# Two graph layers on 32 batches: other first and last work, scalings apart from additions, GpSimd's additions in another order

## The chip, the cores and the metric

The kernel runs on one core of a Trainium2 chip. TensorE (PE) multiplies matrices into PSUM; VectorE (DVE), ScalarE (ACT) and GpSimd (POOL) work on tiles in SBUF; SyncE (SP) and ScalarE issue the transfers. Each engine works through its own list of instructions in order and waits at an instruction until its inputs and its buffer are free. The metric is the device time of one execution in microseconds, lower is better.

## The reference

For 32 batches b, with x[b] of 512 nodes × 512 features and one adjacency matrix for all:

```python
# layer 0: attention with 8 heads of 64, then residual and layer norm
q, k, v = (x @ W + bias).reshape(b, n, 8, 64)        # for Wq, Wk, Wv
scores = einsum('bihd,bjhd->bhij', q, k) / 8
weights = softmax(scores + where(adj == 0, -1e9, 0))
x = layernorm(x + einsum('bhij,bjhd->bihd', weights, v))
# layer 1: graph convolution, then residual and layer norm
deg = adj.sum(axis=1)
norm_adj = adj * deg[:, None]**-0.5 * deg[None, :]**-0.5
x = layernorm(x + norm_adj @ (x @ W1) + b1)
```

## The kernel before

The program is one long list. Every instruction on TensorE, VectorE, ScalarE and GpSimd is pinned to its place (class InOrder), so the code's order is each engine's order; the recording helper is line 44, and the profile puts L44 to nearly everything. Work is therefore told apart by the names of its tiles.

The main loop (746 to 853) goes over S = 128 blocks k. A block is one batch b and one pair g of heads, in the order ORDER = (0, 2, 1, 3). A block makes scores in PSUM (tile sc, TensorE), VectorE subtracts the mask (e<-sc,maskT), ScalarE takes the exponential (e<-e), GpSimd adds the e tiles of a head pair for the denominators (acc<-e and acc<-acc,e, accumulate, 360), and TensorE multiplies e with v (tile av, values, 379). av is transposed by VectorE into yb, and four DMAs set it into the batch's tile YT (name yT; of the last batch wv, which is free by then). The denominators are folded by VectorE (fold, folded) and inverted once per batch (inverse_all: a product with spread, four copies into inv, one RECIPROCAL).

Beside the four blocks of batch b runs the rest, on a list called side: the projections of batch b+1, what finishes batch b-1, and its convolution. Projections use a seven-product scheme (seven, 257): seven products of quarter matrices, each of which VectorE adds to what came before. Their sums go through tiles e1 (name e), u2 (name u) and the outputs v or kq. The products of one scheme go through a PSUM pool of three buffers (name mm). In values_of (286) the fourth product's sum u2 gets the value bias from GpSimd (u<-u,bv_r, in middle), and VectorE's v and the next products' sums follow. x comes as 8 row strips per half (load_x, 105) into a tile that VectorE transposes (turn, 118) to XT; combine makes four differences of it. Weights are loaded as 32-row pieces (load_parts, 146) and get four differences (weigh, 167: wv and wk on GpSimd).

finish (464) scales the values by inv on VectorE (yT<-yT,inv), adds the residual on GpSimd (yT<-yT,xr; both in add, 503), takes mean and variance (measure), their root on GpSimd (rstd), normalises on ScalarE (norm), and splits the result into a high part hi (ScalarE) and a low part lo (VectorE: lo<-yT,dis,hi), both rounded for a faster product; then GpSimd adds b1 (yT<-yT,b_r; both in split, 548). convolve (579) multiplies hi and lo with adjT (first for all batches but the last, block for the last), makes a second seven-product scheme with W1 (second, 623), whose sums extend (660) completes on GpSimd for the batch before the last, then statistics and store.

The dict beside (794 to 800) says which of the finishing work stands behind which of the projection's products; cut deals the list to the four blocks. The second accumulation pair of a block is deferred: it is put on pending, and put_off (more, 741) takes one from there at a place in the list; what is left goes at the head of the next block. So the place of put_off in beside decides where GpSimd's acc<-acc,e stands:

```python
2: put_off, 3: rest[3:4], 4: rest[4:5] + put_off,
```

Product 3 is the one whose sum u2 GpSimd adds the bias to; the number is the position in the list of products, and what is listed there comes behind that product.

Before the loop stand the loads (176 to 192), wv's and wk's differences, the turn of batch 0, its values, the masks (adjacency, 215: transposition of adj by TensorE, a mask, a copy adjT on VectorE, a comparison of the two (off) and its sum (lost)) woven into its keys and queries. Behind the loop come the last batch's late scalings (pairs), the last convolution and stores (855 to 884). The last two blocks take their shares from lines 814 to 823; the last batch's accumulations go into wq, wk, wv and XT, which are free by then.

Of the kernel before, what the change touches and what calls it, by code (L numbers as in the profile page):

```python
# [9 lines left out]
F32 = mybir.dt.float32  # L10
# [39 lines left out]
def unshifted(  # L50
# [54 lines left out]
    def load_x(b, j):  # L105


        if b == 0 and j == 1:
# [9 lines left out]
    def turn(b, j):  # L118
# [4 lines left out]
        if j == 0 and b:  # L123
            load_x(b, 1)

# [20 lines left out]
    def load_parts(w, name, engine):  # L146
        t = consts.tile([P, 7, 2, HALF], F32, name=name)
        for i in range(2):
            for q in range(4):
                engine.dma_start(  # L150
                    t[32 * q : 32 * (q + 1), 2 * i : 2 * i + 2].rearrange("r j u o -> r (j u) o"),
                    w[ts(q, P), ts(i, HALF)].rearrange("(t r) o -> r t o", r=32),
                )
        return t
# [20 lines left out]

    load_x(0, 0)
    load_x(0, 1)
    wv = load_parts(Wv, "wv", nc.scalar)
    bv_r = load_row(bv, "bv_r", nc.scalar)
    bk_c = load_column(bk, "bk_c")  # L180
    bq_c = load_column(bq, "bq_c")
    wk = load_parts(Wk, "wk", nc.sync)
# [9 lines left out]
    b1_r = load_row(b1, "b1_r", nc.sync)  # L192

# [20 lines left out]

    def adjacency(m):
# [6 lines left out]
        vector.tensor_copy(adjT[:, m, :], p)  # L222
        off = work.tile([P, N], F32, name="off", tag="e", bufs=6)
        vector.tensor_tensor(off, p, adjT[:, m, :], ALU.not_equal)
        vector.tensor_reduce(lost[:, m : m + 1], off, AX.X, ALU.add)
# [153 lines left out]
    def values(s):  # L379
# [13 lines left out]
        if jj == 0:  # L393
            return

# [11 lines left out]
        for q in range(4):  # L407
            queue = scalar if q > 1 and (b, g) == blocks[-1] else nc.sync
            queue.dma_start(
# [54 lines left out]
    def finish(b):  # L464
# [38 lines left out]
        def add(i):  # L503
# [5 lines left out]
            gpsimd.tensor_add(y, y, R[b][i])  # L509

        def add_pair(i, g):

            y, r = YT[b][:, i, :], R[b][i]
            for h in (2 * g, 2 * g + 1):
                at = slice(h * HD, (h + 1) * HD)
                vector.scalar_tensor_tensor(
                    y[:, at], y[:, at], t["inv"][:, i, h : h + 1], r[:, at], op0=ALU.mult, op1=ALU.add
                )
# [648 lines left out]
```

## Time and profile before

| | us |
|---|---|
| median of 3 runs | 2893.41 (2891.94 to 2895.27) |
| profiled execution | 2891.81 |
| its span, first to last instruction | 2890.0 |
| TensorE's mean granted clock | 0.995 |
| first block's scores on TensorE start at | 56.83 |
| last block's scores on TensorE start at | 2825.51 |
| one exponential on ScalarE (e<-e, 128x1024) | 1.057 |
| one accumulation on GpSimd (acc<-acc,e) | 2.373 |
| one yT<-yT,inv on VectorE, mean of 124 | 1.216 |
| one yT<-yT,xr on GpSimd, mean of 124 | 1.589 |
| one lo<-yT,dis,hi on VectorE, mean of 124 | 1.272 |

A row of the timeline is start, length, engine, line, operation, output<-inputs with partitions x elements and type, how many in a row were joined, and in brackets the idle time before it and what ended that. Where several are joined, the length is that of the whole row, gaps in it included. PE is TensorE's products, PEld its weight loads. A view of waits has total, number and longest of an engine's idle times by what released it. A row by stages has the stretch, its length, and the busy time of each engine in it with the number of instructions, the granted clock of TensorE as a share of full speed, the share of time that the 16 DMA engines moved data, and GB/s.

### The profile page before, as it was taken

What the parts mean: (1) busy time and instruction counts of PE and PEld (TensorE: products, weight loads), DVE (VectorE), ACT (ScalarE), POOL (GpSimd) and SP (SyncE); (2) the same over time, 40 slices, a digit from 0 to 9 for tenths busy, and PEclk for the clock granted to TensorE, in tenths of its full rate; (3) what the DMA queues carried; (4) which work ended last, traced back from release to release, by engine and by line L of the source; (5) the groups of instructions that cost most, each with busy time, mean ns of one, the idle gap of its engine ahead of it and who ended that gap; (6) DMA issues with size and microseconds to landing.
All of it is one profiled execution on the core that took longest, in us unless ns stands there. A gap on an engine that the chain in (4) does not pass through costs nothing.

```text
span 2890.0 us, 34431 instructions
## 1 busy us (share of the span) xinstructions
PE 2813.2 (97%) x12408; PEld 1867.5 (65%) x12408; DVE 2292.3 (79%) x3205; ACT 1041.4 (36%) x1312; POOL 1844.5 (64%) x1174
## 2 busy tenths in 40 slices
PE   7999999999999999999999999999999999999997
PEld 5566666666666666666666666666666666666655
DVE  6688778788778887787887788877878877888787
ACT  1243333333333433333333334333333333343343
POOL 3566666666666666666666666666666666666665
PEclk9999999999999999999999999999999999999999
DMA  5111222111221112221112211222211122112211
GB/s 131 22 30 48 55 55 44 41 48 48 59 55 41 36 48 55 55 44 41 48 48 59 55 41 35 50 55 55 44 41 48 48 59 56 40 35 50 56 36 53
DMA packets 383396, 142.35 MB, mean 49 GB/s; under 512 B 280048, under 2 KB 349680, under 8 KB 383216
## 3 DMA queue, kind: packets, MB, share of 16 engines
q1 hardware_dynamic: 380720, 138.35, 20.2%
q10 hardware_dynamic: 2496, 1.70, 0.3%
q8 instruction: 100, 1.64, 0.2%
q14 instruction: 80, 0.66, 0.1%
HBM read 72.88 MB, written 33.55 MB: 37 GB/s over the span
## 4 chain that ended last, share of the span: by engine, by line
PE 81%; DVE 11%; POOL 3%; ACT 2%; issue 1%; DMA 0%; SPq 0%; DVEq 0%; POOLq 0%
PE mm L44 49%; PE sc L44 17%; PE av L44 16%; DVE e L44 3%; DVE st L44 2%; ACT y L44 2%; DVE v L44 1%; POOL u L44 1%; POOL rstd L44 1%; DVE mv L44 1%; DVE u L44 1%; DVE yb L44 0%; DVE kq L44 0%; DMA x<-in_x_dram 0%; DVE lo L44 0%
## 5 line engine op out<-in xcount | busy, mean ns | idle before, releaser
L44 ACT ACTIVATE e<-e 128x1024 f32<-128x1024 f32 x512 | 540.7, 1057 | 1164.7 <-DVE e L44 1139.7
L44 POOL TENSOR_TENSOR acc<-acc,e 128x1024 f32<-128x1024 f32 x248 | 588.5, 2373 | 187.3 <-ACT e L44 182.5
L44 DVE SCALAR_TENSOR_TENSOR e<-sc,maskT 128x1024 f32<-128x1024 f32 x512 | 597.5, 1207 | 24.9 <-PE sc L44 24.5
L44 PE MATMUL sc<-kq 64*128 64x512 f32 x2048 | 517.8, 618 | 3.6 <-DVE e L44 3.5
L44 PE MATMUL mm<-xT,wk 128*128 128x256 f32 x1792 | 472.8, 386 | 2.3 <-DVE off L44 1.0
L44 POOL TENSOR_TENSOR acc<-e 128x1024 f32<-128x1024 f32 x126 | 297.1, 2358 | 271.8 <-ACT e L44 271.8
L44 PE MATMUL av<-e,v 128*64 128x512 f32 x2048 | 467.9, 598 | 0.0
L44 PE MATMUL mm<-xT,wq 128*128 128x256 f32 x1792 | 459.9, 379 | 0.0
L44 PE MATMUL mm<-wv,xT 128*128 128x256 f32 x1792 | 408.1, 385 | 49.2 <-DVE e L44 37.9
L44 PEld LDWEIGHTS mm<-wv,xT 128*128 128x128 f32 x1792 | 338.1, 192 | 123.8 <-PE mm L44 33.8
L44 PEld LDWEIGHTS mm<-xT,wk 128*128 128x128 f32 x1792 | 329.8, 190 | 125.6 <-issue 70.1
L44 PEld LDWEIGHTS mm<-xT,wq 128*128 128x128 f32 x1792 | 340.5, 190 | 46.3
L44 PEld LDWEIGHTS sc<-kq 64*128 64x128 f32 x2048 | 173.3, 186 | 284.9 <-issue 156.3
L44 PEld LDWEIGHTS av<-e,v 128*64 128x64 f32 x2048 | 135.5, 136 | 316.2 <-issue 292.4
L44 POOL TENSOR_TENSOR yT<-yT,xr 128x512 f32<-128x512 f32 x124 | 193.4, 1589 | 78.1 <-DVE yT L44 78.1
L44 PE MATMUL mm<-w,zT 128*128 128x256 f32 x992 | 224.6, 379 | 0.0
L44 POOL TENSOR_TENSOR rstd<-ve,minus_half 128x4 f32<-128x4 f32 (+1 forms) x66 | 66.3, 1005 | 243.4 <-DVE nmu L44 243.4
L44 DVE TENSOR_TENSOR kq<-u,mm 128x512 f32<-128x512 f32 x128 | 87.7, 685 | 157.7 <-PE mm L44 154.2
L44 POOL TENSOR_TENSOR yT<-yT,b_r 128x512 f32<-128x512 f32 x124 | 171.5, 1394 | 56.4 <-DVE lo L44 56.4
L44 PEld LDWEIGHTS mm<-w,zT 128*128 128x128 f32 x992 | 188.2, 190 | 27.0 <-issue 1.5
L44 PE MATMUL mm<-adjT,lo 128*128 128x512 f32 x496 | 198.2, 400 | 5.6 <-DVE lo L44 5.6
L44 PE MATMUL mm<-adjT,hi 128*128 128x512 f32 x496 | 203.6, 410 | 0.0
(131 smaller groups left out, 3360.0 us busy)
## 6 DMA issues: line engine op xcount, KB each, us to landing
x<-in_x_dram SPq DMA_DIRECT2D x256, 128.0 KB, 2.9
out_dram<-y SPq DMA_DIRECT2D x127, 256.0 KB, 2.1
xr<-in_x_dram SPq DMA_DIRECT2D x124, 256.0 KB, 3.3
yT<-yb SPq DMA_DIRECT2D x496, 64.0 KB, 2.4
wv<-in_L_gnn_Wv_dram ACTq DMA_DIRECT2D x8, 128.0 KB, 4.8
wk<-in_L_gnn_Wk_dram SPq DMA_DIRECT2D x8, 128.0 KB, 4.1
wq<-in_L_gnn_Wq_dram SPq DMA_DIRECT2D x8, 128.0 KB, 4.8
yT<-in_adj_dram SPq DMA_DIRECT2D x1, 1024.0 KB, 6.8
```

The source lines that it names most:

```text
L44: return self.tc.keep_in_program_order(op(*args, **kwargs))
```

## The change

What it does, in the order of the code. Batch 0 is loaded as four row tiles of 256 KB, which stay as its residual; TensorE turns them by products with the unit matrix (turn_first), copied to XT by VectorE and ScalarE. The pieces of wv go between these tiles, half on SP's queue, half on ScalarE's; both halves of batch 1's x are loaded before the loop. adjacency leaves two copies to ScalarE, and the comparison (compare) goes to the blocks 3 and 4 of the loop. Five of the seven value products of batch 1 go into block 0.

In the steady state add becomes scale and add, and split becomes low and lift: the four scalings are listed ahead of the four additions, the low parts ahead of the additions of b1, and the first two put_off stand behind product 3 and at 5. In the list of instructions of each engine this leaves TensorE, VectorE and ScalarE as they were for batches 2 to 31; on GpSimd one deferred accumulation moves behind the value bias: before acc, u, acc, four yT, after u, acc, acc, four yT.

At the end, the low parts of the batch before the last go ahead of and between other work in the last blocks, and two accumulations are put off behind them (within, and the pending list); the last block's values are copied by ScalarE and VectorE, turned by TensorE into PSUM (turn_values) and read from there by add_pair, without yb and its four DMAs; extend(2) and extend(3) are done at once for all, and the order of the last products of the batch before the last and of the closing list is another.

```diff
@@ -120,8 +120,21 @@
...
-        if j == 0 and b:
+        if j == 0 and b > 1:
...
+    def turn_first(j, i):
+        p = ps_mm.tile([P, 2, HALF], F32, name="mm")
+        for n in range(2):
+            for u in range(2):
+                for q in range(4):
+                    at = q * P + (2 * i + u) * 32
+                    tensor.matmul(
+                        p[32 * q : 32 * (q + 1), u, ts(n, P)], R[0][2 * j + n][:, at : at + 32], ident,
+                        start=True, stop=True,
+                    )
+        (scalar.copy if i else vector.tensor_copy)(XT[:, 2 * j + i], p)
     def combine(b, at):
@@ -173,13 +188,19 @@
...
-    load_x(0, 0)
-    load_x(0, 1)
-    wv = load_parts(Wv, "wv", nc.scalar)
-    bv_r = load_row(bv, "bv_r", nc.scalar)
+    R[0] = acts.tile([P, NT, D], F32, name="xr", tag="zT", bufs=1)
+    R[0] = [R[0][:, i, :] for i in range(NT)]
+    wv = consts.tile([P, 7, 2, HALF], F32, name="wv")
+    for i in range(2):
+        for k, engine in enumerate((nc.sync, nc.scalar)):
+            engine.dma_start(R[0][2 * i + k], x[0, ts(2 * i + k, P), :])
+            load_parts(Wv, "wv", engine, wv, [(i, 2 * k), (i, 2 * k + 1)])
+        if i == 0:
+            bv_r = load_row(bv, "bv_r", nc.scalar)
+    wk = load_parts(Wk, "wk", nc.sync)
...
-    wk = load_parts(Wk, "wk", nc.sync)
@@ -190,6 +211,9 @@
...
+    if B > 1:
+        load_x(1, 0)
+        load_x(1, 1)
@@ -212,6 +236,8 @@
...
+    plainT = acts.tile([P, NT, N], F32, name="plainT", tag="hi", bufs=1)
     def adjacency(m):
@@ -219,10 +245,13 @@
...
-        vector.tensor_copy(adjT[:, m, :], p)
-        off = work.tile([P, N], F32, name="off", tag="e", bufs=6)
-        vector.tensor_tensor(off, p, adjT[:, m, :], ALU.not_equal)
-        vector.tensor_reduce(lost[:, m : m + 1], off, AX.X, ALU.add)
+        scalar.copy(adjT[:, m, :], p)
+        scalar.copy(plainT[:, m, :], p)
+    def compare(m):
+        vector.tensor_tensor(plainT[:, m, :], plainT[:, m, :], adjT[:, m, :], ALU.not_equal)
+        vector.tensor_reduce(lost[:, m : m + 1], plainT[:, m, :], AX.X, ALU.add)
@@ -392,6 +421,12 @@
...
+        if (b, g) == blocks[-1]:
+            turned = work.tile([P, N], F32, name="avT", tag="yb", bufs=1)
+            scalar.copy(turned[:, :HALF], av[:, :HALF])
+            vector.tensor_copy(turned[:, HALF:], av[:, HALF:])
+            AV[b, g] = turned
+            return
@@ -405,8 +440,7 @@
...
-            queue = scalar if q > 1 and (b, g) == blocks[-1] else nc.sync
-            queue.dma_start(
+            nc.sync.dma_start(
@@ -500,21 +534,31 @@
...
-        def add(i):
+        def scale(i):
...
-            gpsimd.tensor_add(y, y, R[b][i])
+        def add(i):
+            gpsimd.tensor_add(YT[b][:, i, :], YT[b][:, i, :], R[b][i])
+        def turn_values(g):
+            t["y"] = ps_mm.tile([P, NT, P], F32, name="mm")
+            for i in range(NT):
+                tensor.transpose(t["y"][:, i], AV[b, g][:, ts(i, P)], ident)
         def add_pair(i, g):
...
-            for h in (2 * g, 2 * g + 1):
+            for k in range(2):
+                h = 2 * g + k
...
+                values = t["y"][:, i, ts(k, HD)] if (b, g) == blocks[-1] else y[:, at]
...
-                    y[:, at], y[:, at], t["inv"][:, i, h : h + 1], r[:, at], op0=ALU.mult, op1=ALU.add
+                    y[:, at], values, t["inv"][:, i, h : h + 1], r[:, at], op0=ALU.mult, op1=ALU.add
...
         def measure(i):
@@ -545,12 +589,13 @@
...
-        def split(i):
-            x1 = YT[b][:, i, :]
+        def low(i):
...
-                LO[b][i], x1, dis[:, i : i + 1], HI[b][:, i, :], op0=ALU.mult, op1=ALU.subtract
+                LO[b][i], YT[b][:, i, :], dis[:, i : i + 1], HI[b][:, i, :], op0=ALU.mult, op1=ALU.subtract
...
-            gpsimd.tensor_add(x1, x1, b1_r)
+        def lift(i):
+            gpsimd.tensor_add(YT[b][:, i, :], YT[b][:, i, :], b1_r)
         def grow(i):
@@ -560,11 +605,11 @@
...
-            early=[(0.6, inverse, ((0,),))], late=[(0.6, inverse, ((1,),))],
+            early=[(0.6, inverse, ((0,),))], late=[(0.6, inverse, ((1,),)), (0.6, turn_values, (ORDER[-1],))],
...
-            inverse=[(0.6, inverse_all, ())], add=block(add), measure=block(measure), root=[(0, root, ())],
-            judge=[(0, judge, ())], norm=block(norm), split=block(split), grow=block(grow),
+            inverse=[(0.6, inverse_all, ())], scale=block(scale), add=block(add), measure=block(measure), root=[(0, root, ())],
+            judge=[(0, judge, ())], norm=block(norm), low=block(low), lift=block(lift), grow=block(grow),
...
     def weave(side, main):
@@ -639,13 +684,11 @@
...
-                if not aside:
-                    extend(2)
+                extend(2)
...
-                if not aside:
-                    extend(3)
+                extend(3)
@@ -710,7 +753,7 @@
...
-            extend=[(0, extend, (k,)) for k in range(2, 7)],
+            extend=[(0, extend, (k,)) for k in range(4, 7)],
@@ -743,60 +786,72 @@
...
+    put_off = [(0, more, ())]
...
-    run(sum(turns(0), []))
...
+    first = values_of(0)
+    turn_first(0, 0)
+    turn_first(0, 1)
+    run(first[:1])
+    value_biases()
+    turn_first(1, 0)
+    turn_first(1, 1)
+    combine(0, 0)
+    combine(0, 1)
+    run(first[1:2])
+    combine(0, 2)
+    combine(0, 3)
...
-    first = values_of(0)
-    run(first[:2])
-    value_biases()
+    run(first[2:])
...
-    if B > 1:
-        load_x(1, 0)
-    run(first[2:])
+    wq_parts = [(0, weigh_part, (wq, vector, k)) for k in range(4)]
+    first = keys_and_queries(0, 0)
+    run(wq_parts[:2] + first[:1] + wq_parts[2:3] + first[1:2] + wq_parts[3:] + first[2:])
...
-    first = keys_and_queries(0, 0)
-    run(first[:1])
-    weigh(wq, vector)
-    run(first[1:])
...
-    shares, rest = [], []
+    shares, rest, within = [], [], []
...
-            if 0 < b < B - 1:
+            if 1 < b < B - 1:
...
-                main, kq = values_of(b + 1) + keys_and_queries(b + 1, 0), keys_and_queries(b + 1, 1)
+                main, kq = keys_and_queries(b + 1, 0), keys_and_queries(b + 1, 1)
+                if b:
+                    main = values_of(b + 1) + main
...
-                side = main[:7] + [(0, degrees, ())] + weave(w1_parts, main[7:]) + turn0 + kq[5:] + turn1
-                shares = cut(side, (6, 5, 5, 5))
-                for share in shares:
-                    share[1:1] = [(0, more, ())]
-                    share[4:4] = [(0, more, ())]
+                exact = [(0, compare, (m,)) for m in range(NT)]
+                main += kq[5:]
+                beside = {
+                    2: put_off, 3: [(0, degrees, ())] + put_off, 6: put_off, 7: w1_parts[:1] + put_off,
+                    8: w1_parts[1:2], 9: turn0 + w1_parts[2:3], 10: put_off + exact[:2], 11: put_off + w1_parts[3:],
+                    12: exact[2:], 13: turn1,
+                }
+                side = early[5:6] + put_off + early[6:] + put_off
+                side += sum(([piece] + beside.get(i, []) for i, piece in enumerate(main)), [])
+                shares = cut(side, (4, 4, 4, 4))
...
-                norm, split, grow = f["norm"], f["split"], f["grow"]
-                add, measure = f["add"], f["measure"]
-                put_off = [(0, more, ())]
+                norm, low, grow, measure = f["norm"], f["low"], f["grow"], f["measure"]
...
-                    0: rest[:1], 1: rest[1:3], 2: put_off, 3: rest[3:4], 4: rest[4:5] + put_off,
-                    5: rest[5:6] + f["inverse"], 6: rest[6:] + add[:2], 7: add[2:],
+                    0: rest[:1], 1: rest[1:3], 3: rest[3:4] + put_off, 4: rest[4:5],
+                    5: rest[5:6] + f["inverse"] + put_off, 6: rest[6:] + f["scale"][:2], 7: f["scale"][2:] + f["add"],
...
-                    12: norm[1:2] + split[:1], 13: norm[2:3] + split[1:2], 14: norm[3:] + split[2:3],
-                    15: split[3:], 16: put_off + grow[:2], 17: put_off + grow[2:], 18: turn0 + f["judge"],
+                    12: norm[1:2] + low[:1], 13: norm[2:3] + low[1:2], 14: norm[3:] + low[2:3],
+                    15: low[3:] + f["lift"], 16: put_off + grow[:2], 17: put_off + grow[2:], 18: turn0 + f["judge"],
@@ -808,16 +863,17 @@
...
-                    add = last["add"]
-                    side += h[:1] + last["inverse"] + h[1:2] + add[:2] + h[2:3] + add[2:]
+                    scale, add = last["scale"], last["add"]
+                    side += h[:1] + last["inverse"] + h[1:2] + scale[:2] + h[2:3] + scale[2:] + add
...
-                s, first, norm, split, pairs = c["second"], c["first"], f["norm"], f["split"], last["pairs"]
+                s, first, low, lift, pairs = c["second"], c["first"], f["low"], f["lift"], last["pairs"]
+                within = low[:1]
...
-                    h[3:4] + f["measure"] + f["root"] + h[6:] + norm + f["judge"],
-                    h[4:6] + split + last["early"] + first[:2] + held["measure"][:2] + first[2:3]
-                    + held["measure"][2:] + first[3:] + c["parts"] + f["grow"],
+                    h[3:4] + f["measure"] + f["root"] + h[6:] + f["norm"] + f["judge"],
+                    h[4:5] + low[1:3] + h[5:6] + low[3:] + lift + put_off + put_off + last["early"] + first[:2]
+                    + held["measure"][:2] + first[2:3] + held["measure"][2:] + first[3:] + c["parts"] + f["grow"],
@@ -829,6 +885,10 @@
...
+        if k == 0:
+            run(two)
+            early = values_of(1)
+            run(early[:2])
@@ -838,7 +898,11 @@
...
-        if k < S:
+        if k == S - 2:
+            run(within)
+            scores((*blocks[k], 1))
+            pending += [((*blocks[k], jj),) for jj in range(2)]
+        elif k < S:
@@ -848,17 +912,17 @@
...
-            run(two)
+            run(early[2:3] + put_off + early[3:4] + put_off + early[4:5])
...
-    norm, split, block, pairs, extend = end["norm"], end["split"], e["block"], end["pairs"], c["extend"]
-    run(end["late"] + s[2:3] + pairs[2] + held["store"] + s[3:4])
-    run(sum((pairs[3][i : i + 1] + end["measure"][i : i + 1] for i in (0, 1)), []) + end["halves"][:1] + s[4:5])
-    run(sum((pairs[3][i : i + 1] + end["measure"][i : i + 1] for i in (2, 3)), []) + end["halves"][1:] + s[5:6])
-    run(norm[:2] + split[:1] + block[:1] + extend[:2] + norm[2:3])
-    run(split[1:2] + block[1:2] + extend[2:4] + norm[3:] + split[2:3] + block[2:3] + split[3:] + block[3:] + end["judge"])
+    norm, low, lift, block, pairs, extend = end["norm"], end["low"], end["lift"], e["block"], end["pairs"], c["extend"]
+    run(end["late"][:1] + pairs[2] + end["late"][1:] + s[2:3] + held["store"])
+    run(sum((pairs[3][i : i + 1] + end["measure"][i : i + 1] for i in (0, 1)), []) + end["halves"][:1] + s[3:5])
+    run(sum((pairs[3][i : i + 1] + end["measure"][i : i + 1] for i in (2, 3)), []) + extend[:1] + end["halves"][1:])
+    run(s[5:6] + norm[:2] + low[:1] + block[:1] + low[1:2] + block[1:2] + lift[:1] + extend[1:2] + norm[2:] + low[2:3])
+    run(block[2:3] + low[3:] + lift[1:2] + block[3:] + lift[2:] + end["judge"])
@@ -873,7 +937,7 @@
...
-    run(e["unload"] + e["parts"] + s[6:] + end["grow"] + extend[4:] + c["measure"][:2])
+    run(e["unload"] + e["parts"] + s[6:] + end["grow"] + extend[2:] + c["measure"][:2])
```

More of the change, by code (lines that the diff above doesn't have):

```diff
@@ L105, in load_x @@
     def load_x(b, j):
-        if b == 0 and j == 1:
+        if b == 1 and j == 1:
             X[b, j] = work.tile([P, 8, DT, 32], F32, name="x1", tag="e", bufs=6)
@@ L144, in load_residual, with load_parts @@
             nc.sync.dma_start(R[b][i], x[b, ts(i, P), :])
[L146 to L153, printed above, removed]
+    PIECES = [(i, q) for i in range(2) for q in range(4)]
+    def load_parts(w, name, engine, t=None, pieces=PIECES):
+        if t is None:
+            t = consts.tile([P, 7, 2, HALF], F32, name=name)
+        for i, q in pieces:
+            engine.dma_start(
+                t[32 * q : 32 * (q + 1), 2 * i : 2 * i + 2].rearrange("r j u o -> r (j u) o"),
+                w[ts(q, P), ts(i, HALF)].rearrange("(t r) o -> r t o", r=32),
+            )
         return t
```

## The prediction

> **What bounds the kernel now.** I read the page's totals first, then TensorE's waits, then busy time by stage, and last the timeline of the places that the waits name.
>
> ```profile
> span 2890.0 us, 34431 instructions
> PE 2813.2 (97%) x12408; PEld 1867.5 (65%) x12408; DVE 2292.3 (79%) x3205; ACT 1041.4 (36%) x1312; POOL 1844.5 (64%) x1174
> ```
> TensorE is busy for 97%. No change to the additions can win more than its 77 us of idle time and what it loses at a lower clock. So the question is where those lie. The waits of TensorE over the whole span:
>
> ```profile
> PE mm L44 <- DVE e L44: 37.9, 32, 5.3
> PE mm L44 <- DVE xT L44: 12.6, 3, 9.3
> PE mm L44 <- DVE lo L44: 5.6, 4, 2.6
> PE sc L44 <- DVE e L44: 3.5, 3, 2.8
> PE sc L44 <- ACT hi L44: 3.3, 1, 3.3
> ```
> (total, times, longest). Limited to 279.8 to 2754.5 us the view leaves one line, 28.1 us in 28 waits of 1.0: one per batch. The rest lies at the two ends. Busy time by stage (length, then PE, PEld, DVE, ACT, POOL, granted clock, DMA share, GB/s):
>
> ```profile
> 1340.40:1428.80 88.40, 87.35 (x387) 58.12 (x388) 70.65 (x99) 32.50 (x41) 57.46 (x37) 1.00 0.20 48
> 0.00:57.00 57.00, 41.27 (x186) 34.54 (x188) 37.97 (x52) 4.87 (x6) 14.43 (x23) 1.00 0.66 148
> 57.00:103.00 46.00, 37.65 (x151) 21.19 (x152) 32.02 (x34) 13.52 (x14) 25.09 (x13) 0.93 0.18 35
> 2800.00:2826.00 26.00, 20.44 (x82) 12.60 (x80) 19.24 (x23) 11.74 (x16) 12.17 (x9) 0.80 0.07 10
> ```
> The first line is one batch of the steady state: 1.05 us of idle in 88.40. The other three lose 16, 8 and 6 us, two of them at a clock below 1. The steady wait in the timeline:
>
> ```profile
> 1390.49 2.36 POOL L44 TENSOR_TENSOR acc<-acc,e 128x1024 f32<-128x1024 f32 x1
> 1390.90 0.69 DVE L44 TENSOR_TENSOR u<-e,mm 128x512 f32<-128x512 f32 x1 [1.04 <-PE mm L44]
> 1392.81 1.27 POOL L44 TENSOR_TENSOR u<-u,bv_r 128x512 f32<-128x512 f32 x1
> 1394.04 2.36 POOL L44 TENSOR_TENSOR acc<-acc,e 128x1024 f32<-128x1024 f32 x1
> 1394.12 0.69 DVE L44 TENSOR_TENSOR v<-u,mm 128x512 f32<-128x512 f32 x1 [2.52 <-POOL u L44]
> 1395.55 1.97 PE L44 MATMUL mm<-wv,xT 128*128 128x256 f32 x8 [1.00 <-DVE e L44]
> 1396.82 0.35 DVE L44 RECIPROCAL inv<-inv 128x32 f32<-128x32 f32 x1
> 1398.15 4.64 DVE L44 TENSOR_TENSOR yT<-yT,inv 128x512 f32<-128x512 f32 x4
> ```
> VectorE makes u by 1391.59. GpSimd is in an accumulation until 1392.85 and adds the bias only then. VectorE's v, its e behind it, and the seventh value product (k = 6), which needs the PSUM buffer that e frees, follow late: 1.00 us. The two ends:
>
> ```profile
> 13.15 6.28 POOL L44 TENSOR_TENSOR wv<-wv 128x512 f32<-128x512 f32 x4 [10.87 <-DMA wv<-in_L_gnn_Wv_dram]
> 82.57 8.08 PE L44 MATMUL mm<-wv,xT 128*128 128x256 f32 x24 [5.31 <-DVE e L44]
> 2808.28 2.36 POOL L44 TENSOR_TENSOR wq<-e 128x1024 f32<-128x1024 f32 x1 [7.95 <-ACT e L44]
> 2808.58 8.74 DVE L44 SCALAR_TENSOR_TENSOR lo<-yT,dis,hi 128x512 fp32r<-128x512 f32 x4
> 2811.25 0.50 PE L44 MATMUL mm<-adjT,lo 128*128 128x512 f32 x1 [2.64 <-DVE lo L44]
> ```
>
> **What the Trainium skill says.** "SBUF — State Buffer", section "Who interferes with whom": a VectorE instruction with two SBUF inputs and a GpSimd instruction that reads SBUF exclude each other; whichever starts first holds the shared ports for its whole length. The trace agrees: of the yT scalings, which read two SBUF tiles, those alone take 0.68 us, those under a GpSimd addition 1.75; the first lo above lasted until the accumulation ended. Operations with one SBUF and one PSUM input (v, e, kq) show 0.69 in either case, as the page has it. "VectorE: DVE Perf Modes", section "First, the fixed hardware budget", calls the reciprocal an iterative divide; its 0.35 us on 32 elements, against 0.17 for a plain operation of that size, fits. "TensorE: Matmul & The Clock Gate", section "Part 1: The HAM clock gate (the "warmup" mystery)": about 3.4 us without work halves TensorE's clock. After the 5.31 us wait above, 24 products took 8.08 us against 5.45 at 71.81. At 2812 to 2822, after waits of 2.64 and 1.99, convolution products came every 0.43 us, not every 0.233.
>
> **The steady state (batches 2 to 31), part by part.** Splitting the scaling from its addition, and the low part from the lift (the b1 addition), changes no order on any engine there: each yT addition still waits for its own scaling and VectorE issues the same list. These edits cost and gain nothing. One thing moves: with one deferred accumulation fewer ahead of it, GpSimd's bias addition comes before the two accumulations, not between them. Both still end before their readers ask.
>
> Gain: u is added at 1391.65 to 1392.92 instead of 1392.81 to 1394.08; v and e follow 1.15 earlier (v at 1392.97, e's end 1394.25), and the seventh product starts at about 1394.4 for 1395.55.
>
> Loss: the second accumulation runs 1395.2 to 1397.56, not 1394.04 to 1396.40. With v(k6) also earlier, VectorE comes to the first scaling at about 1397.0 and is locked out until 1397.56. Before, it started at 1398.15. From there VectorE has no idle time until TensorE's next wait for it (0.45 us at 1415.54, for u of the keys), so this chain is early by 0.6 to 0.65 only, and TensorE waits there for the other half microsecond.
>
> Net 0.65 us. Over the 29 such waits: 19 us. Ends: 13 (0.45 each, if a second lock takes 0.2) and 33 (1.15 each, if something later has slack).
>
> **The start.** Batch 0 is loaded as four row tiles that serve as its residual too, turned by 64 products and four copies in place of two stream transposes. wv's pieces interleave with it on SP's and ScalarE's queues, and wk follows on SP's.
>
> wv's factors begin on GpSimd at 13.15 now, when the last piece is there. About 0.3 MB of wk then no longer shares the queues' 210 GB/s (worked out for the first 25 us), so about 1.5 us earlier; wv and wk's factors (6.28 + 5.68 us) then end at 23.5 and the bias addition follows at once, where it waited 1.49 more for u. The first key product, which came 2.74 after that addition (29.43 − 26.69), starts at 26.2: −3.2. The new copies and turning lie beside these 12 us of GpSimd. Cover gone, they cost about 2 us (bound 0 to 3).
>
> The adjacency's second copy and comparison (off, lost) leave VectorE there; TensorE's 0.98 wait for off and two small ones go: −1.3. First scores at 52.3 instead of 56.83: −4.5.
>
> Blocks 0 and 1 wait 2.84 + 0.20 + 0.54 + 5.31 us and lose 2.9 to the clock after it: 11.8. Value products of batch 1 now stand between the scores of block 0, and the 5.31 goes with the clock loss, since those products no longer queue behind block 1's softmax. I keep 2.8 of it: −9.
>
> The four comparisons go to blocks 3 and 4, now with both inputs in SBUF (0.68, 1.75 at worst, plus a 0.69 reduction): 5.5 to 9.8 us on a VectorE that is busy for 70%. Cost 1.5 (0 to 4).
>
> Sum −12 (−8 to −16).
>
> **The tail.** The first low part goes ahead of the block's second scores, the next ones between convolution pieces, and the two accumulations into wq and wk behind them. So lo no longer waits for 2808.28 to 2813.4: the waits of 2.64, 1.99, 0.47 and 0.47 and their pitch go, 7.1 us by the end of the first low tile row, and 1.75 more of half clock: 8.9. The last block's values are copied by ScalarE and VectorE and turned by TensorE, dropping a transpose (0.71) and four DMAs (2.65 from issue to landing): 1.5 earlier at the last hi; two more extend additions on GpSimd ahead of the second root cost 0.5. Sum −10 (−7 to −12).
>
> **The sum**: −19 − 12 − 10 = −41. The profiled execution took 2891.81 us (span 2890.0), so 2850.8; the runs' median, 2893.41, lies 1.6 above it: 2852.
>
> **Rivals.**
>
> B, the reciprocal is locked out. It never ran beside a GpSimd operation before; it now falls at about 1395.7, under the second accumulation. If it takes both ports it ends at 1397.9, v(k6) comes 0.35 later than before and so does the chain: +10 for −19. For: inv's plain neighbour low took 0.99 under an accumulation, 0.17 alone. Against: an iterative divide at 0.35 isn't in a two-port mode. −12 − 10 + 10: 2881.
>
> C, the lock costs nothing downstream, since the chain has slack that I don't see: 1.15 each, −33 − 22: 2838. Against: no VectorE gap from 1398 to 1415.
>
> D, slower. The same lock at the first scaling: two accumulations back to back end past 1398.8 (e late, or the yT additions pushed behind a scaling each), and the chain to 1415 comes late in every batch. It decides from 0.76 us lost per batch (22 of the ends over 29); at 1.0 the result is 2900. Against: all 248 accumulations took 2.36 to 2.4.
>
> The move in the steady state is no gain at all: the wait reappears whole at 1415.54; only the ends count: 2871. It is the upper end of the forecast's own range.
>
> **Numbers.** Forecast 0.67 (its own range 2834 to 2872), C 0.16, B 0.11, D 0.05, something below 2832 0.01. The range 2832 to 2872 takes in the ends' bounds and C, and leaves out B and D. A measurement of this kernel tells 0.2% (5.8 us) from no change. Faster 0.92 (forecast, C and most of B), same 0.03, slower 0.05.
>
> **What would show it.** Right: GpSimd's u ahead of both accumulations and v some 1.3 us after its start; the 28 waits of 1.0 gone and the wait at the key product near 0.9 instead of 0.45; the first yT scaling starting as the accumulation ends; first scores near 52; no stretch of half clock near 2810; four lo of under 1 us. Wrong: a reciprocal above 1 us (B), a period of 87.3 (C) or over 88.4 (D), or an early stage whose TensorE waits for row tiles or copies of turned x.

## The result, and the profile after

The changed kernel takes 2856.57 us (median of 4 runs, 2855.78 to 2858.47) against 2893.62 before (4 runs, 2891.94 to 2895.27): 37 us or 1.3% less, ratio 0.9873 with a 95% interval of 0.9856 to 0.989. The forecast was 2852. The profiled execution was the longest of the four, 2858.47 us with a span of 2856.4; the execution profiled before, 2891.81, was shorter than each of the four timed ones. So the two profiles stand 33.3 us apart, the medians 37.1.

The totals of the changed kernel's profile:

```profile
span 2856.4 us, 34678 instructions
PE 2817.5 (99%) x12540; PEld 1865.2 (65%) x12540; DVE 2301.6 (81%) x3201; ACT 1046.8 (37%) x1323; POOL 1846.0 (65%) x1174
```
TensorE's idle time fell from 77 to 39 us, while its busy time rose by 4 (132 more instructions, which turn batch 0 and the last values). VectorE's busy time rose by 9, although it has four instructions fewer: time in which it is locked out counts as busy.

TensorE's waits over the whole span (total, times, longest):

```profile
PE mm L44 <- DVE u L44: 11.3, 30, 0.4
PE mm L44 <- DMA xr<-in_x_dram: 4.7, 1, 4.7
PE sc L44 <- DVE e L44: 3.3, 1, 3.3
PE sc L44 <- ACT hi L44: 2.2, 1, 2.2
PE mm L44 <- issue: 2.0, 1, 2.0
```
The 28 waits of 1.0 us for e are gone. In their place, at another product, stand 30 of 0.38 us for u, the key products' sum. Before, TensorE hardly waited there. By stages (columns as before): one steady batch, then three stretches of the start.

```profile
1340.05:1427.85 87.80, 87.42 (x389) 57.96 (x388) 71.23 (x98) 32.49 (x41) 57.52 (x37) 1.00 0.21 49
0.00:55.20 55.20, 47.04 (x312) 39.83 (x312) 27.27 (x42) 10.34 (x16) 14.33 (x23) 0.97 0.60 143
55.20:98.20 43.00, 42.38 (x185) 25.59 (x184) 32.53 (x36) 13.52 (x14) 25.04 (x13) 1.00 0.14 25
127.30:154.05 26.75, 23.49 (x100) 15.23 (x99) 22.36 (x32) 4.23 (x4) 15.18 (x10) 0.94 0.15 31
```
The batch went from 88.40 to 87.80. Blocks 0 to 2 (the third row here, against 57 to 103 before) have lost almost all idle time. Block 5, the last row, has gained some: 3.3 us idle and a clock of 0.94. The timeline of the steady state, with VectorE and GpSimd, and TensorE's new wait:

```profile
1376.11 0.69 DVE L44 TENSOR_TENSOR u<-e,mm 128x512 f32<-128x512 f32 x1 [1.04 <-PE mm L44]
1376.88 1.27 POOL L44 TENSOR_TENSOR u<-u,bv_r 128x512 f32<-128x512 f32 x1 [1.14 <-DVE u L44]
1378.11 4.80 POOL L44 TENSOR_TENSOR acc<-acc,e 128x1024 f32<-128x1024 f32 x2
1378.18 0.69 DVE L44 TENSOR_TENSOR v<-u,mm 128x512 f32<-128x512 f32 x1 [1.38 <-POOL u L44]
...
1381.07 0.35 DVE L44 RECIPROCAL inv<-inv 128x32 f32<-128x32 f32 x1
1381.62 0.69 DVE L44 TENSOR_TENSOR v<-e,mm 128x512 f32<-128x512 f32 x1 [0.19 <-PE mm L44]
1382.22 5.18 DVE L44 TENSOR_TENSOR yT<-yT,inv 128x512 f32<-128x512 f32 x4
...
1383.53 6.24 POOL L44 TENSOR_TENSOR yT<-yT,xr 128x512 f32<-128x512 f32 x4 [0.63 <-DVE yT L44]
...
1400.14 1.13 PE L44 MATMUL mm<-xT,wk 128*128 128x256 f32 x4 [0.38 <-DVE u L44]
```
The bias addition starts as soon as u is there, and v waits 1.38 instead of 2.52. The two accumulations last until 1382.91. The first scaling could start at 1382.22 and is held until then: the four take 5.18 us, where they took 4.64.

Set against the start of its batch, the seventh value product now comes 1.14 us earlier than before (median of batches 4 to 30). TensorE gives back 0.33 of that at the wait above. Another 0.13 and 0.09 go at two products ahead of it, one of scores and one of keys. These come late without a gap that the list of waits shows.

Where the time went is best read from the times at which the first scores of a block start on TensorE (block 0, 5, 6, 16, 124, 127) and the span, in us. Batches 4 to 30 lie between block 16 and block 124.

| kernel | 0 | 5 | 6 | 16 | 124 | 127 | span |
|---|---|---|---|---|---|---|---|
| before | 56.83 | 139.33 | 161.85 | 382.70 | 2768.96 | 2825.51 | 2890.0 |
| changed | 55.24 | 127.27 | 154.05 | 374.27 | 2744.83 | 2793.09 | 2856.4 |
| e1, bias first alone | 57.52 | 141.34 | 163.87 | 384.08 | 2754.53 | 2810.95 | 2875.5 |
| e2, bias between again | 53.32 | 125.35 | 152.01 | 372.81 | 2759.00 | 2807.22 | 2869.9 |
| e3, lo behind again | 55.27 | 127.31 | 154.31 | 374.49 | 2745.07 | 2800.98 | 2864.9 |
| e4, last values by DMA | 53.23 | 125.25 | 151.98 | 372.17 | 2742.25 | 2790.49 | 2854.4 |
| e5, first scaling no lock | 53.38 | 125.41 | 152.14 | 370.66 | 2725.98 | 2774.21 | 2837.2 |
| e6, accumulation moved on | 53.37 | 125.41 | 152.41 | 371.22 | 2729.25 | 2777.50 | 2840.7 |
| e7, no comparisons | 53.58 | 125.61 | 147.37 | 367.52 | 2737.78 | 2786.01 | 2849.0 |
| e8, bias 0 on VectorE | 50.90 | 122.93 | 150.99 | 371.14 | 2741.39 | 2789.63 | 2852.6 |
| e9, comparisons spread | 54.33 | 130.27 | 152.02 | 372.21 | 2742.81 | 2791.06 | 2853.9 |
| e10, e6 + e8 + e9 | 51.24 | 127.02 | 148.78 | 367.59 | 2725.59 | 2773.32 | 2836.5 |
| e11, e10, comparisons later | 52.05 | 124.05 | 146.95 | 365.76 | 2723.76 | 2771.99 | 2835.3 |

Of the 33.6 us between the two spans, 8.4 are won by block 16, 15.7 more from there to block 124 (0.58 in each of 27 batches), 8.3 in blocks 124 to 126, and 1.2 behind them. Of the changed kernel's profiles with the same start (the row above and e2 to e6), two start the first scores at 55.2 and four at 53.2 to 53.4; the profile here is one of the late two. Two pairs differ before block 16 in the start alone: before and e2, 9.9 us apart at block 16, and e1 and e4, 11.9.

### The profile page after: what moved, and what is told of

It is laid out like the page before. It is cut to its first block, busy times and chain, and to the rows that moved or that the text cites. A ratio compares the mean times of both kernels' runs of the same rounds, so it can differ in the third digit from the quotient of the medians.

```text
span 2856.4 us, 34678 instructions
## 1 busy us (share of the span) xinstructions
PE 2817.5 (99%) x12540; PEld 1865.2 (65%) x12540; DVE 2301.6 (81%) x3201; ACT 1046.8 (37%) x1323; POOL 1846.0 (65%) x1174
## 3 DMA queue, kind: packets, MB, share of 16 engines
q8 instruction: 101, 1.65, 0.2%
## 4 chain that ended last, share of the span: by engine, by line
PE 78%; DVE 19%; issue 2%; POOL 0%; DMA 0%; ACT 0%; DVEq 0%; POOLq 0%; ACTq 0%
PE mm L44 52%; PE sc L44 13%; PE av L44 12%; DVE yT L44 5%; DVE e L44 5%; DVE st L44 3%; DVE acc L44 1%; DVE u L44 1%; DVE mv L44 1%; DVE yb L44 1%; DVE v L44 1%; DVE kq L44 1%; DVE xT L44 0%; DVE plainT L44 0%; POOL xT L44 0%
## 5 line engine op out<-in xcount | busy, mean ns | idle before, releaser
L44 POOL TENSOR_TENSOR yT<-yT,b_r 128x512 f32<-128x512 f32 x124 | 171.2, 1392 | 63.3 <-DVE lo L44 63.3
```

The lines of the kernel that those rows point to most:

```text
L44: return self.tc.keep_in_program_order(op(*args, **kwargs))
```

## The experiments

All were timed in three rounds beside the kernel before, whose median lay between 2891.94 and 2893.32 in these rounds. The changed kernel was not timed again in them; ratios are to the kernel before, and two kernels are called different where their intervals don't meet or where the table above shows the place.

**e1: the bias first, alone.** The kernel before, with two places of the list changed:

```diff
-0: rest[:1], 1: rest[1:3], 2: put_off, 3: rest[3:4], 4: rest[4:5] + put_off,
-5: rest[5:6] + f["inverse"], 6: rest[6:] + add[:2], 7: add[2:],
+0: rest[:1], 1: rest[1:3], 3: rest[3:4] + put_off, 4: rest[4:5],
+5: rest[5:6] + f["inverse"] + put_off, 6: rest[6:] + add[:2], 7: add[2:],
```


> The kernel before with one edit: in batches 2 to 31 GpSimd's value bias goes ahead of both deferred accumulations; start and end as before. My theory, that the accumulation behind it locks the first scaling out and so gives about half of the won 1.15 us back: 0.6 us less per batch, 30 batches, about 18 us less than before (2875 of 2893). Rival 1, nothing is given back: 33 less (2860). Rival 2, all is given back, and the changed kernel won only at its two ends: no difference (2893).

Measured 2876.41 us, 15.5 less than before (0.9943, 0.9927 to 0.996). From block 16 to block 124 it gains 15.8. Both rivals fall: the gain is neither 33 nor nothing.

**e2: the bias between the accumulations again**, the same edit taken out of the changed kernel.

> The changed kernel with this one edit taken back (bias between the two accumulations again), its new start and end kept, scalings and additions still listed apart. My theory: 18 us more than the changed kernel, 2875, since listing scalings and low parts apart changes no engine's order. Rival, that the apart listing carries part of the gain: less than 12 us more.

Measured 2873.20 (0.9934, 0.9917 to 0.9951), 16.6 more than the changed kernel. From block 16 to block 124 it takes 2386.20, before 2386.26. So listing the scalings and low parts apart carries nothing in the steady state; the place of the bias carries all of it.

**e3: the low parts behind the accumulations again.**

```diff
-within = low[:1]
+within = []
-h[4:5] + low[1:3] + h[5:6] + low[3:] + lift + put_off + put_off + last["early"] + first[:2]
+h[4:6] + low + lift + last["early"] + first[:2]
-        if k == S - 2:
-            run(within)
-            scores((*blocks[k], 1))
-            pending += [((*blocks[k], jj),) for jj in range(2)]
-        elif k < S:
+        if k < S:
```


> The changed kernel with the two accumulations of the block before the last ahead of the low parts again, and the low parts together behind the block's scores; the rest of the new end kept. My theory: TensorE's waits of 2.6 and 2.0 us for lo and the half clock behind them come back, 8 to 9 us more (2865). Rival, that the last block would have waited for GpSimd's b1 additions anyway: 3 us or less.

Measured 2865.06 (0.9904, 0.9888 to 0.9921), 8.5 more. Its timeline, of the accumulations, lo and the products that wait:

```profile
2784.68 2.35 POOL L44 TENSOR_TENSOR wq<-e 128x1024 f32<-128x1024 f32 x1 [7.96 <-ACT e L44]
2784.96 8.74 DVE L44 SCALAR_TENSOR_TENSOR lo<-yT,dis,hi 128x512 fp32r<-128x512 f32 x4
2787.00 2.80 POOL L44 TENSOR_TENSOR wk<-e 128x1024 f32<-128x1024 f32 x1
2787.64 0.50 PE L44 MATMUL mm<-adjT,lo 128*128 128x512 f32 x1 [2.65 <-DVE lo L44]
2790.40 0.80 PE L44 MATMUL mm<-adjT,lo 128*128 128x512 f32 x1 [2.03 <-DVE lo L44]
...
2795.63 0.63 PE L44 MATMUL mm<-adjT,lo 128*128 128x512 f32 x1
...
2796.93 0.40 PE L44 MATMUL mm<-adjT,lo 128*128 128x512 f32 x1
```
The picture of before is back: four lo in 8.74 us, two waits of 2.65 and 2.03, and after the second the products are longer, 0.63 to 0.80, until 2796. In the changed kernel three of the four lo take 0.73 to 0.75 us and one 1.19. One wait of 0.91 is left, and the products take 0.40 behind it:

```profile
2787.05 0.50 PE L44 MATMUL mm<-adjT,lo 128*128 128x512 f32 x1 [0.91 <-DVE lo L44]
2787.39 0.40 PE L44 MATMUL mm<-adjT,hi 128*128 128x512 f32 x1
```
This is the half clock that the Trainium skill describes in "TensorE: Matmul & The Clock Gate", section "Part 1: The HAM clock gate (the "warmup" mystery)". The page has it come after about 3.4 us of idle; here it came with waits of 2.65 and 2.03 us, and the measurement decides. The last section says what the traces show of it.

**e4: the last values by transposition and DMA again** (the two copies, turn_values and the reading from PSUM taken out).

> The changed kernel with the last block's values transposed by VectorE and moved by four DMAs again, in place of two copies and four products into PSUM; the rest of the new end kept. My theory: the values come about 1.5 us later and the end with them, 1 to 3 us more. Rival, the way through DMA lies beside the other last products and costs nothing: within 0.5 us.

Measured 2857.50 (0.988, 0.9864 to 0.9896), 0.9 more; the intervals overlap widely. In the table the stretch from block 127 to the end is 63.9 instead of 63.3 us. The direction is that of the theory, but neither the theory nor its rival is settled by this: the profile of e4 has 6.8 us of half clock from 2817.5 on, where that of the changed kernel has 3.4 from 2822.5 on. Half speed for 3.4 us more can cost up to 1.7, which is more than the difference.

**e5: a first scaling that can't be locked out.**

```diff
             y = YT[b][:, i, :]
+            if i == 0 and b < B - 2:
+                return vector.transpose(y, y)
             vector.tensor_mul(
```


> The changed kernel with the first of the four scalings of each batch 0 to 29 replaced by a transposition in place of the same tile, which has one SBUF input and about the same length; the scaling of that row tile is left out, so the output is not the reference's. My theory, that the second accumulation locks this scaling out for 0.6 us and that VectorE's chain from there to TensorE's wait of 0.38 us per batch has no slack: the transposition starts under the accumulation, the wait goes from 0.38 to 0, 30 x 0.38 = 11 us less than the changed kernel (2845 of 2856.6). Rival, the chain is bound by the later scalings against the residual additions: the lock moves one scaling on, 3 us or less.

This kernel leaves out the scaling of one row tile in batches 0 to 29. Measured 2839.06 (0.9817, 0.9801 to 0.9834), 17.5 less than the changed kernel. Its timeline of VectorE at that place:

```profile
1371.22 0.35 DVE L44 RECIPROCAL inv<-inv 128x32 f32<-128x32 f32 x1
1371.76 0.69 DVE L44 TENSOR_TENSOR v<-e,mm 128x512 f32<-128x512 f32 x1 [0.19 <-PE mm L44]
1372.37 0.70 DVE L44 STREAM_TRANSPOSE yT<-yT 128x512 f32<-128x512 f32 x1
1373.00 4.00 DVE L44 TENSOR_TENSOR yT<-yT,inv 128x512 f32<-128x512 f32 x3
```
The transposition runs its 0.70 us under the accumulation, where the scaling took 1.23. The batch falls from 87.798 to 87.234 us: 0.56, where the scaling had been drawn out by 0.55. At all three products where TensorE gave back 0.33, 0.13 and 0.09 it now gives back nothing. The gain was larger than I expected, since I took the 0.38 us of TensorE's wait for all there was to win. Against before, the batch is now 1.146 us shorter, and 1.15 was the worked-out gain of the bias's move without a lock.

**e6: the second accumulation behind two residual additions**, nothing left out:

```diff
-5: rest[5:6] + f["inverse"] + put_off, 6: rest[6:] + f["scale"][:2], 7: f["scale"][2:] + f["add"],
+5: rest[5:6] + f["inverse"], 6: rest[6:] + f["scale"][:2],
+7: f["scale"][2:] + f["add"][:2] + put_off + f["add"][2:],
```


> The changed kernel with the second accumulation behind the first two residual additions (GpSimd: bias, accumulation, two additions, accumulation, two additions); nothing is left out. My theory: the first two scalings start unlocked, so VectorE's chain is earlier by up to 0.6 us; the third meets an addition as it does now; 11 us less than the changed kernel at most (2845 to 2850). Rival: the last scaling now meets the 2.36 us accumulation instead, and the lock is the same or longer: 2857 to 2866.

Measured 2843.03 (0.9829, 0.9813 to 0.9846), 13.5 less than the changed kernel. Its timeline:

```profile
1369.95 2.37 POOL L44 TENSOR_TENSOR acc<-acc,e 128x1024 f32<-128x1024 f32 x1
1374.06 4.65 DVE L44 TENSOR_TENSOR yT<-yT,inv 128x512 f32<-128x512 f32 x4
1374.83 3.33 POOL L44 TENSOR_TENSOR yT<-yT,xr 128x512 f32<-128x512 f32 x2 [2.51 <-DVE yT L44]
1378.12 2.82 POOL L44 TENSOR_TENSOR acc<-acc,e 128x1024 f32<-128x1024 f32 x1
1380.97 1.25 DVE L44 STREAM_TRANSPOSE acc<-acc 128x1024 f32<-128x1024 f32 x1
```
GpSimd is free when the scalings begin, and they take 4.65 us again. Now it is GpSimd that is held: the accumulation is issued at 1378.12, has to wait for the last scaling and takes 2.82 instead of 2.37. The rival, that the lock only moves on to a scaling, falls. TensorE's waits between 280 and 2720 us are an empty list in e5 and e6. The list leaves out gaps under 0.15 us, though. The batch of e6 (87.334) is still 0.1 longer than that of e5, and the 0.1 lies at the key product of the old wait: its gap is 0.38 us in the changed kernel, 0.14 in e6 and 0.04 in e5 (medians of batches 4 to 30). It fits the moved accumulation: VectorE's transposition of such sums (acc<-acc) starts 0.03 us after it has ended and 0.08 later in the batch than in e5, and VectorE is late by 0.1 from there to the key product.

**e7: without the comparisons.**

```diff
-10: put_off + exact[:2], 11: put_off + w1_parts[3:],
-12: exact[2:], 13: turn1,
+10: put_off, 11: put_off + w1_parts[3:],
+13: turn1,
```


> The changed kernel without the four comparisons of adjT with its unrounded copy and their sums (a zero stands in the count instead; the copies by ScalarE stay). My theory: they cost what the trace shows at 136.1, a 3.3 us wait of TensorE for the masked scores, and about 1 us of half clock behind it: 4 us less than the changed kernel (2852.5). The forecast's term for them was 1.5, which is the rival.

Measured 2850.69 (0.9855, 0.9839 to 0.9872), 5.9 less. (All four comparisons stand in block 4 of the program's list; the text on the change and the forecast put them in blocks 3 and 4.) In the table block 5 falls from 26.78 to 21.76 us, so 5.0 are theirs. What they did in the changed kernel, in its timeline of the end of block 4 and of block 5 (rows of VectorE and TensorE):

```profile
122.99 2.28 DVE L44 TENSOR_TENSOR plainT<-plainT,adjT 128x512 f32<-128x512 f32 x1
...
125.91 2.12 DVE L44 TENSOR_TENSOR plainT<-plainT,adjT 128x512 f32<-128x512 f32 x1
...
134.86 2.32 DVE L44 SCALAR_TENSOR_TENSOR e<-sc,maskT 128x1024 f32<-128x1024 f32 x2
136.10 3.68 PE L44 MATMUL sc<-kq 64*128 64x512 f32 x8 [3.26 <-DVE e L44]
```
VectorE goes through comparisons and key sums without a gap until 134.86, and only then masks the scores that TensorE had ready at 129.2. TensorE waits 3.26 us, and then runs its eight products in 3.68 instead of 1.99: the wait and 1.7 us of half clock make the 5.0. The comparisons and their sums are 8.5 us of work (the first two took 2.28 and 2.12, the others 0.68 each). In e7 VectorE's gaps from 111.2 to the same masks, at 127.49, are 0.85, 0.44 and 1.04, together 2.3 us: too few for them.

**e8: the bias of batch 0 on VectorE.**

```diff
-gpsimd.tensor_add(u2, u2, bv_r[:, None, HALF:].to_broadcast([P, 2, HALF]))
+(gpsimd if b else vector).tensor_add(u2, u2, bv_r[:, None, HALF:].to_broadcast([P, 2, HALF]))
```


> The changed kernel with the value bias of batch 0 alone added by VectorE, not by GpSimd, where it stands behind the differences of wv and wk until 24.18. My theory: TensorE's 2.0 us gap before the first key product closes to under 1 us, and so does the half clock of about 1.7 us behind it: 3 to 4 us less than the changed kernel (2853). Rival: the query half waits for ScalarE's scaling of wq, which ends at 24.4, and little is won: 1 us.

Measured 2853.93 (0.9866, 0.985 to 0.9883), 2.6 less; the intervals overlap, the trace shows the place. TensorE's timeline at the first key products, first of the changed kernel, then of e8:

```profile
26.85 1.97 PE L44 MATMUL mm<-xT,wk 128*128 128x256 f32 x4 [2.04 <-issue]
28.62 1.89 PE L44 MATMUL mm<-xT,wq 128*128 128x256 f32 x4
30.32 1.04 PE L44 MATMUL mm<-xT,wk 128*128 128x256 f32 x4
```
```profile
24.27 1.03 PE L44 MATMUL mm<-xT,wk 128*128 128x256 f32 x4
25.13 1.03 PE L44 MATMUL mm<-xT,wq 128*128 128x256 f32 x4
```
In the changed kernel a gap of 2.04 us is followed by two groups at about half speed. In e8 both are gone, the keys begin 2.6 earlier, and the first scores at 50.90. Block 5 gives 1.3 of it back (28.06 us instead of 26.78): TensorE's wait for the masks is 3.26 as before, but the half clock with it lasts 6.8 us instead of 3.4, and the 48 value products behind take 11.81 instead of 10.63.

The half clock also makes the two groups of start times above. The gap before the first key product is 2.0 to 2.2 us in all six profiles; half clock follows it in the two late ones and in none of the four early ones. Of an early one, e2:

```profile
26.61 1.10 PE L44 MATMUL mm<-xT,wk 128*128 128x256 f32 x4 [2.20 <-issue]
27.55 1.03 PE L44 MATMUL mm<-xT,wq 128*128 128x256 f32 x4
```

**e9: the comparisons one by one in blocks 1 and 2** (exact[:1], [1:2], [2:3], [3:] behind key products 0, 1, 4, 5).

> The changed kernel with its four comparisons one each behind the key products 0, 1, 4 and 5 of batch 1 (blocks 1 and 2), where VectorE waits for TensorE about 1 us in each product, in place of two and two in block 4. My theory: leaving them out won 5.9 us, of which most is the place, not the work: 4 to 5.5 us less than the changed kernel (2851.5). Rival: they lock against GpSimd's accumulations and weight differences there too and cost as much: 2855 to 2858.

Measured 2855.35 (0.9869, 0.9853 to 0.9886), 1.2 less, with overlapping intervals: this falls to the rival. Block 5 is as short as without them (21.75), but blocks 0 to 4 take 75.94 instead of 72.03. TensorE's wait, in its timeline:

```profile
104.89 3.21 PE L44 MATMUL sc<-kq 64*128 64x512 f32 x8 [2.00 <-DVE e L44]
```
It is the same wait, for masked scores, two blocks earlier. My premise of a gap of 1 us per product was wrong there. In e7, which has no comparisons, VectorE goes from 93.22 to beyond 103 without a gap, since the sum of adj over its rows (2.28 us) stands there too; the last two comparisons fall into that stretch.

**e10: e6, e8 and e9 together.**

> The changed kernel with the second accumulation behind two residual additions, the comparisons spread and the value bias of batch 0 on VectorE. If the three are independent, their single gains add up: 13.5 + 2.6 + about 5 = 21 less than the changed kernel (2835.5). If the earlier start only moves VectorE's lag to block 5, less than 17.

Measured 2838.48 (0.9811, 0.9794 to 0.9827), 18.1 less than the changed kernel. The single gains as measured, 13.5 + 2.6 + 1.2, make 17.3: the three add up within the spread of the runs, and the forecast of 21 was too high by what e9 fell short.

**e11: e10 with the comparisons in block 5's value products** (`rest = exact` at the end of batch 0's list, which the next batch takes as it takes the statistics later).

> The kernel of e10 with one edit: the four comparisons stand behind the value products 0, 1 and 3 of batch 2 (block 5), the place that the statistics of an earlier batch take from the next batch on. My theory, that a comparison costs TensorE's time only where VectorE has no gap in the block: VectorE waits 1.0 us for each product there, so nearly the whole price goes, 3 to 4.5 us less than e10 (2834.5). Rival, that VectorE's two-input comparisons are locked out by GpSimd and delay the sums there as well: 2838 or more.

Measured 2836.72 (0.9807, 0.9791 to 0.9823). From e10 it differs by 1.8 in the medians, with overlapping intervals: less than the forecast of 3 to 4.5, and short of the rival's 2838. In the trace blocks 0 to 5 together take 94.90 instead of 97.54; without comparisons and with the changed kernel's start they took 93.79. So 1.1 of the 5.0 are left: the comparison at 140.05 draws out the bias addition to 1.65 us and TensorE waits 1.01 once. e11 is the shortest kernel here and computes all that the changed one does: 57 us less than before.

## Why the prediction was right, and where its terms were off

**Bound and stages.** The reading held: TensorE bounds the kernel, the steady loss is one wait per batch, the rest lies at the ends. The gain came from all three, 16, 10 to 12 and 9.5 us, against the forecast's 19, 12 and 10. The steady state and the low parts were undone by themselves. Of the start only the sum and two costs were measured: what the row tiles, the masks and the value products in block 0 each bring was not tried.

**Steady state, −19.** The mechanism was right at each step: edits with no change of order gave nothing (e2); the bias's move is worth 1.15 a batch (e5); the lock on the first scaling takes half of it back (e5, e6). Measured 0.58 a batch for 0.65, and 15.5 to 16.6 us in e1 and e2. The lock was worked out from the Trainium skill, "SBUF — State Buffer", section "Who interferes with whom": a VectorE instruction with two SBUF inputs and a GpSimd instruction that reads SBUF shut each other out. The traces agree: the two-input scaling took 1.23 under an accumulation, the one-input transposition 0.70, and in e6 it is GpSimd that waits. One sign was misread: the 0.45 us that I took for TensorE's wait at 1415.54 was that of its weight loads. It went to 0.78, and TensorE's own wait from a gap of 0.04 to one of 0.38.

**Rival B** (the reciprocal locked out) fell by the profile, without an experiment: 0.35 us under the accumulation at 1381.07, as when free. **C** (no cost of the lock) and **D** (a cost above the gain) fell with the period of 87.80. D's premise, that an accumulation could end past the equivalent of 1398.8, did not occur. **The fourth** (the wait reappears whole) fell as well, but a part of it did reappear, as forecast.

**Start, −12.** Measured 9.9 and 11.9 in the two pairs that differ in it alone, but that this is near 12 is in part luck, since errors met. The first key product came at 26.85 for 26.2. The half clock behind the gap before it, which I had not counted, makes 1.7 us where it occurs: the first scores are at 55.24 with it and at 53.2 to 53.4 without, not at 52.3. The 64 products that turn batch 0 stand in the trace as 128 instructions. Blocks 0 to 4 gained 10.5 (82.50 to 72.03), where I had 9 for blocks 0 and 1. The comparisons are the term that failed: I costed them as 1.5 on a VectorE that is busy for 70%, and they cost 5.0 to 5.9 (e7). The share fits the stretch 57 to 103 of the kernel before (32.02 of 46.00 us), in which TensorE itself lost 8 us. In blocks 3 and 4 TensorE has no gap, and VectorE is busy there for 23.12 of 29.04 us without the comparisons (e7), 80%. What decides is the 2.3 us of gaps ahead of the next masks, for 8.5 us of work. My bound of 4 did not hold it, and 1.75 as the worst length of one comparison did not either (2.28).

**Tail, −10.** Measured −8.3 for the low parts (forecast 8.9; e3 gives 8.5) and −1.2 for the rest (forecast 1.5 less 0.5; e4 gives 0.9, not clear from zero).

**The sum** was 4 us too optimistic against the medians (−41 for −37), of which some 3 lie in the steady state.

## What to carry to other kernels

Before moving an addition of GpSimd ahead to free one waiter, write down which VectorE instructions then stand beside the instruction that comes behind it; those with two SBUF inputs pay with the overlap, and it may be enough to move the long GpSimd instruction once more, behind the short ones (e6: 13.5 us for two edited lines). A wait that TensorE's view shows at a new place can understate what is to be won there; the period of the loop is the better measure. Work on an engine that is "busy for 70%" isn't free: in the stretch where the work is put, add up the gaps between its place and the next instruction that TensorE waits for.

## What I had not expected of the hardware

Neither of two waits of 2.65 and 2.03 us is long by itself, but in e3 the products of lo and hi after them came 0.43 us apart, not 0.233, for some 6 us. A single gap of 2.04 us was followed by half speed for 3.4 us in the changed kernel's start, and one of 2.20 in e2 was not.

The traces show an order in this. In each of the 13 profiles the stretches at half clock begin on a grid of 3.413 us: in the changed kernel at 26.94, 136.16, 2822.45 and 2849.76, which are 32, 787 and 8 steps apart. All but each profile's last one, which runs into the end, last one, two or three steps. Three steps of the changed kernel, then two of e2, by stages:

```profile
23.52:26.93 3.41, 1.37 (x8) 0.90 (x6) 1.46 (x3) 0.90 (x1) 1.91 (x2) 1.00 1.08 371
26.93:30.34 3.41, 3.41 (x9) 2.70 (x10) 3.30 (x8) 0.00 (x0) 0.00 (x0) 0.50 1.16 235
30.34:33.75 3.41, 3.41 (x17) 3.02 (x16) 1.31 (x3) 0.84 (x2) 0.00 (x0) 1.00 0.87 145
24.77:28.18 3.41, 1.56 (x7) 1.44 (x8) 2.87 (x8) 0.00 (x0) 0.42 (x1) 1.00 1.08 365
28.18:31.59 3.41, 3.41 (x17) 3.00 (x16) 3.08 (x5) 0.84 (x2) 0.00 (x0) 1.00 1.23 185
```
In the changed kernel the whole gap falls into one step, TensorE is idle for 2.04 of 3.41 us, and the next step has half clock. In e2 the grid cuts the longer gap, 1.85 us fall into the second step, and the clock stays. Over all 13 profiles, from where their record of the clock begins (8 to 15 us into the span), each step at full clock with 1.99 us or more of idle was followed by half clock, and each with 1.92 or less by full clock. The ends of products are modelled, so this border is rough. In e3 the two waits put 2.7 us of idle into one step; in the kernel before the first wait alone put 2.64 there. So what counts in these traces is the idle time in a step, not the length of one wait, and where the grid lies differs from execution to execution.

And a VectorE instruction can hold up GpSimd as well as the reverse (accumulation of 2.82 for 2.37, bias addition of 1.65 for 1.27), which made a reordering cheap, since GpSimd had time at that place.
